# Another layout for the table of relative destinations in a graph-layer kernel, and two short VectorE operations put ahead of a long one

## The chip, the cores and the metric

The kernel runs on one core of a Trainium2 chip. The metric is the device time of one execution in microseconds (us). The kernel before was timed three times: 261.72, 261.30 and 260.92 us, median 261.3 us. Five engines work side by side, each through its own list of instructions in order: TensorE (PE, with its weight loads shown apart as PEld), VectorE (DVE), ScalarE (ACT), GpSimd (POOL) and SyncE (SP), which issues most of the DMA transfers here. They wait for each other through semaphores.

## The reference

The layer adds up edge features by destination node and puts each node through a small network:

```python
recv = edge_index[1]                                  # dst, sorted, 412500 edges
agg = jax.ops.segment_sum(edges, recv, num_segments=12500)   # edges: 412500 x 48
u = graph_globals[batch]                              # batch is 0 for every node
h0 = jnp.maximum(_layernorm(x), 0.0)                  # x: 12500 x 128
h = jax.nn.relu(jnp.concatenate([h0, agg, u], axis=1) @ W1 + b1)   # 240 -> 256
out = x + h @ W2 + b2                                 # 256 -> 128
```

All of it is float32. The edges come sorted by destination, with random counts for each node.

## The kernel before, in words

**Tiling.** The edges are cut into 538 chunks of 768 (128 partitions of 6 consecutive edges each; T = 6 is the place in the partition). Four chunks (CG = 4) make a group and 11 groups (GI = 11) an iteration, which also takes 1024 nodes. There are 12 iterations (NIT), one extra group ahead of them and a rest behind.

**Segment sum by matmuls.** For each edge the kernel keeps its destination relative to the middle of its chunk's window, the table `rel`: one column for each chunk and each of the six places. In each iteration VectorE copies the 264 numbers that it will need (11 groups of 24) from `rel` into the small tile `rel_i` (operation `fr`, in the helper `fetch`), makes one-hot matrices from it by comparing with a row of 28 numbers (`oh0` to `oh5`, in the helper `onehot`, 1344 columns each, one of 672), and TensorE multiplies them with the edge features (`su0` to `su5`, L739). ScalarE copies each result out of its PSUM bank (`ss0` to `ss5`). The results alternate between two banks, so `su5` can only begin when ScalarE has done `ss3`. A second set of one-hots (`pl`) puts the sums at their nodes (`pc`).

**The nodes.** VectorE makes the layer norm's statistics (`st`, `sm`) and shifts (`sh`), ScalarE the normalised rows (`xn`, 8 instructions in an iteration), TensorE turns them (`tu`, L798) and runs the two layers (`hh` L808, `ha` L813, `w2` L834). On ScalarE's list `ss3` stands behind `xn`, and `xn` waits for VectorE's `sh`.

**The start.** Before the loop the destinations are loaded in five blocks of 128 chunks, with a chunk in each partition. VectorE makes them relative (`df`), TensorE transposes them, three places at a time, through three PSUM banks in turn (`td`, L620), and ScalarE copies each turned piece into `rel` (`cd`, L621). The middles of the blocks come from small matmuls (`of`, L613) and two VectorE operations (`vv`, L629, and `off`, L631, in the helper `dst_3`), for block 0 first and for blocks 1 to 4 together later. VectorE also makes the bias (`bj`) from a small matmul (`bi`).

**What sets the order.** Each engine's order is the order in which the program names the operations. A small planner adds the waits: an operation waits for the writers of what it reads, unless its engine already knows of them by a wait for something later on the same engine. What TensorE's loop needs of work ahead of the loop and doesn't learn by its own waits in the loop, it waits for once, at the loop's entry.

Of the kernel before, what the change touches and what calls it, by code (L numbers as in the profile page):

```python
# [18 lines left out]
P = 128  # L19
EPS = 1e-5  # L20
T = 6
CE = P * T
CG = 4
GE = CG * CE
GI = 11
# [29 lines left out]
class Flow:  # L55
# [14 lines left out]
    def op(self, eng, name, reads, writes, emit, dma=False, late=None):  # L70
        self.seq.append(dict(eng=eng, name=name, r=tuple(reads), w=tuple(writes), emit=emit, dma=dma, it=self.at, late=late or {}))
# [350 lines left out]
def kernel(  # L422
# [12 lines left out]
    nc = tc.nc  # L435
# [5 lines left out]
    NIT = E // IE  # L441
    NCH = -(-E // CE)
# [9 lines left out]
    q = CG * T  # L452
# [4 lines left out]
    const = sbufs.enter_context(tc.tile_pool(name="const", bufs=1))  # L457
# [11 lines left out]
    lead = const.tile([P, LEAD], F32)  # L469
    wide = [const.tile([P, len(p) * CG, ROW], F32, name=f"e{s}") for s, p in enumerate(SLOTS)]  # L470
    e = [w[:, :, :T * DE] for w in wide]
    rel = const.tile([P, ((NIT + 1) * GI + 1) * q], F32)
    off = const.tile([P, (NIT + 1) * GI + 1], F32)
    worst = const.tile([P, 3], F32)
    far = const.tile([P, 1], F32)
    farm = const.tile([P, 1], F32)
    rel_i = const.tile([P, GI, q], F32)
    off_i = const.tile([P, GI], F32)
    oh = [const.tile([P, len(p) * q, V], F32, name=f"oh{s}") for s, p in enumerate(SLOTS)]
# [54 lines left out]
    op = f.op  # L534
    A, B, Z = 0, 1, 2

    def dma(eng, name, reads, writes, dst_ap, src_ap):
        def emit(i):
            with nc.allow_non_contiguous_dma(reason="small pieces"):
                return [f.of[eng].dma_start(dst_ap(i) if callable(dst_ap) else dst_ap, src_ap(i) if callable(src_ap) else src_ap)]  # L540
        op(eng, name, reads, writes, emit, dma=True)
# [52 lines left out]
    def dst_shape(b):  # L594
        rows = min(P, NCH - b * P)
        return rows, min(P // CG, NG - b * P // CG), b * P // CG
# [12 lines left out]
    def dst_2(b):  # L609
        rows, n, g0 = dst_shape(b)  # L610
        ob, ok = (ph[1], "PH1") if b else (S[0][:, P:], "S0")
        op("PE", f"of{b}", [f"mf{b}", "aq"], [ok], lambda i: [
            nc.tensor.matmul(ob[:, g0:g0 + n], aq[:rows].rearrange("c k n -> c (k n)"), mf[b][:rows, :n], start=True, stop=True, skip_group_check=True)])  # L613
        dv = df[b % DF].rearrange("c (p t) -> c t p", t=T)
        rv = rel[:, b * P * T:(b * P + rows) * T].rearrange("p (c t) -> p t c", t=T)
        for t0 in range(0, T, 3):
            key, bk = (("PT", pt), ("PH0", ph[0]), ("PO", po))[(2 * b + t0 // 3) % 3]
            pv = bk[:, :3 * P].rearrange("p (t c) -> p t c", t=3)
            op("PE", f"td{b}.{t0}", [f"df{b % DF}", "ident"], [key],
               lambda i, t0=t0, pv=pv: [nc.tensor.transpose(pv[:, t, :rows], dv[:rows, t0 + t, :], ident[:rows, :rows]) for t in range(3)])  # L620
            op("ACT", f"cd{b}.{t0}", [key], [f"rel{b}.{t0}"], lambda i, t0=t0, pv=pv: [nc.scalar.copy(rv[:, t0:t0 + 3], pv[:, :, :rows])])  # L621

    def dst_3(bk, key, some):

        g0 = some[0] * (P // CG)
        n = min(NG, (some[-1] + 1) * (P // CG)) - g0
        vs = [f"vv{b}" for b in some]
        op("DVE", f"vv{some[0]}", [key, "base"], vs, lambda i: [
            nc.vector.tensor_tensor(vv[:, g0:g0 + n], bk[:, g0:g0 + n], flat[:, g0:g0 + n], OP.subtract)])  # L629
        op("DVE", f"of{some[0]}x", vs + ["nmod"], [f"off{b}" for b in some], lambda i: [  # L630
            nc.vector.tensor_scalar(off[:, g0:g0 + n], vv[:, g0:g0 + n], nmod, (WIN - V) / 2, OP.add, OP.add)])  # L631
# [29 lines left out]
    def cols(ap, i, a, n):  # L661
        return ap[:, ds(a(i), n)] if not isinstance(i, int) else ap[:, a(i):a(i) + n]

    def fetch(j):

        it = (f.at or 0) + j
        g0, g1 = it * GI + 1, min(NG, (it + 1) * GI + 1)
        m = GI * CG
        blocks = [b for b in range(NB) if b * P < g1 * CG and (b + 1) * P > g0 * CG]
        rv = rel_i.rearrange("p g t -> p (g t)")  # L670

        op("DVE", "fr", ["relz"] + [f"rel{b}.{t0}" for b in blocks for t0 in (0, 3)], ["rel_i"], lambda i: [nc.vector.tensor_scalar(
            rv, cols(rel, i, lambda i: ((i + j) * GI + 1) * q, m * T), 0.0, None, OP.add)])

    def fetch_off(j):
        it = (f.at or 0) + j
        g0, g1 = it * GI + 1, min(NG, (it + 1) * GI + 1)
        blocks = [b for b in range(NB) if b * P < g1 * CG and (b + 1) * P > g0 * CG]
        op("DVE", "fo", ["offz"] + [f"off{b}" for b in blocks], ["off_i"], lambda i: [nc.vector.tensor_scalar(
            off_i, cols(off, i, lambda i: (i + j) * GI + 1, GI), 0.0, None, OP.add)])  # L680

    def onehot(name, o, reads, r):

        k, n = r.shape[1], r.shape[2]
        ov = o.rearrange("p (k n) v -> p k n v", k=k)
        op("DVE", f"oh{name}", reads + ["iota_v"], [f"oh{name}"], lambda i: [nc.vector.tensor_tensor(  # L686
            ov, iota_v[:, None, None, :].to_broadcast([P, k, n, V]), r[:, :, :, None].to_broadcast([P, k, n, V]), OP.is_equal)])
# [6 lines left out]
    def onehots(s):  # L694
        g = SLOTS[s]
        onehot(s, oh[s], ["rel_i"], rel_i[:, g[0] - 1:g[0]] if len(g) == 1 else rel_i[:, g[0] - 1:g[1]:g[1] - g[0]])
# [149 lines left out]
    def prologue():  # L846
# [12 lines left out]
        pool = lambda name, w, fn, r=(): op("POOL", name, r, w, lambda i: [fn()])  # L859
# [15 lines left out]
        dma("POOL", "lw1b", [], ["w1b"], w1a[HI:HI + DE], W1[D:D + DE])  # L875
        dma("POOL", "lw2", [], ["w2"], w2, W2.rearrange("(a p) d -> p a d", p=P))
        dma("POOL", "lb2", [], ["b2"], b2_sb, b2[None, :].to_broadcast([P, D]))
        pool("relz", ["relz"], lambda: nc.gpsimd.memset(rel[:, NCH * T:], 0.0))

        op("DVE", "c0", [], ["eps", "zero", "worst1", "worst2"], lambda i: [  # L880
            nc.vector.memset(zero, 0.0), nc.vector.memset(eps, EPS), nc.vector.memset(worst, 0.0)])
# [16 lines left out]
        for b in range(NB):  # L898
            dst_1(b)
            dst_2(b)  # L900
        dst_3(S[0][:, P:], "S0", [0])
        onehot(5, oh[5][:, q:], ["rel0.0", "rel0.3"], rel[:, :q].rearrange("p (g t) -> p g t", g=1))
        op("PE", "su5", ["oh5", "e5.1"], ["S1"], lambda i: [
            nc.tensor.matmul(S[1][NV * c:NV * c + V, DE:2 * DE], oh[5][:, (CG + c) * T + t], e[5][:, CG + c, t * DE:(t + 1) * DE],
                             start=(t == 0), stop=(t == T - 1), skip_group_check=True)
# [5 lines left out]
        onehots(1)  # L911
        op("PE", "bi", ["w1u", "u"], ["PH1"], lambda i: [
            nc.tensor.matmul(ph[1][:, NG + a:NG + a + 1], w1u[:, a * P:(a + 1) * P], u, start=True, stop=True, skip_group_check=True) for a in range(NH)])
        onehots(2)
        op("DVE", "bj", ["PH1", "b1"], ["bias"], lambda i: [nc.vector.tensor_tensor(bias, ph[1][:, NG:NG + NH], b1_sb, OP.add)])
        dst_3(ph[1], "PH1", range(1, NB))
        fetch_off(1)
        op("DVE", "spare", [], ["spare"] + [f"di{b}" for b in range(NB)] + [f"di{NB - 1}r", f"di{NB - 1}s"] + [f"df{k}" for k in range(DF)],
           lambda i: [nc.vector.memset(hold[0][:, 0:1], 0.0)])
# [3 lines left out]
            places(s)  # L923
        places_near()
        split("plf", plf, far_, ["off0"], lambda j: off[:, 0:1])
        op("DVE", "f0", ["rel0.0", "rel0.3"], ["farm"], lambda i: [nc.vector.tensor_reduce(farm, rel[:, :q], AX.X, OP.max, apply_absolute_value=True)])

    def body(it):
        f.at = it
# [140 lines left out]
```

## Time and profile before

| | |
|---|---|
| median of three runs | 261.3 us |
| the profiled execution | 261.09 us |
| its span, first to last instruction | 259.3 us |
| PE, DVE, ACT busy | 237.5, 237.4, 128.6 us |
| DMA, mean rate over the span | 364 GB/s |
| from one iteration to the next | 18.16 us |
| `fr`, 264 numbers | 298 ns, 13 times |
| ScalarE's copy of 384 numbers into `rel` | about 0.9 us, 8 times |

The span has three parts: a start to about 34 us, twelve iterations, and an end from about 243 us. Two engines are busy over nine tenths of the time, and the DMA engines move about 390 GB/s through the iterations, so the shares alone do not tell which of them sets the period.

### The profile page before, as it was taken

The numbers are of one execution on the slowest core, as the hardware profiler recorded it, in microseconds if no ns is written. First come the engines' busy times: TensorE is split into PE (matmuls) and PEld (weight loads), VectorE is DVE, ScalarE is ACT, GpSimd is POOL, SyncE is SP. The second block draws the span as 40 slices with busy tenths as digits, with TensorE's granted clock in tenths as the row PEclk, the third lists the DMA queues.
The fourth block names the chain that finished last, engine by engine and source line by source line (L and its number), as shares of the span: only waits on it lengthen the run. The fifth ranks groups of instructions, "written<-read, shape, count | busy, mean of one in ns | idle before, by whom it ended". The sixth has DMA issues, their size and how long they took to land.

```text
span 259.3 us, 17135 instructions
## 1 busy us (share of the span) xinstructions
PE 237.5 (92%) x7539; PEld 185.9 (72%) x7540; DVE 237.4 (92%) x643; ACT 128.6 (50%) x326; POOL 9.1 (4%) x23
## 2 busy tenths in 40 slices
PE   0864889999999999999999999999999999999990
PEld 0854765976967958949859769679589498597680
DVE  5799999999999999999999999999999999999640
ACT  4630454644645536646546446455366465564520
POOL 8200020000000000000000000000000000000000
PEclk9997599999999999999999999999999999999999
DMA  6999999999999999999999999999999999959951
GB/s 215 285 380 388 364 389 391 390 392 390 390 392 390 391 392 390 391 392 390 390 393 390 393 389 391 392 385 388 393 382 389 393 385 390 393 210 350 364 223 65
DMA packets 79012, 94.33 MB, mean 364 GB/s; under 512 B 3227, under 2 KB 72189, under 8 KB 78998
## 3 DMA queue, kind: packets, MB, share of 16 engines
q1 hardware_dynamic: 75398, 87.63, 94.6%
q10 hardware_dynamic: 3312, 6.03, 6.1%
q0 software_dynamic: 288, 0.49, 0.7%
q8 instruction: 7, 0.11, 0.2%
q14 instruction: 7, 0.06, 0.1%
HBM read 87.75 MB, written 6.40 MB: 363 GB/s over the span
## 4 chain that ended last, share of the span: by engine, by line
PE 86%; DVE 6%; DMA 2%; issue 2%; ACT 1%; SPq 0%; DVEq 0%
PE s L739 26%; PE ph L834 17%; PE ph L808 9%; PE ax L761 7%; PE ph L813 5%; PE po L808 4%; PE pt L808 4%; PE pt L813 4%; DVE oh L686 3%; PE pt L798 3%; DMA holda<-in_dst_dram 2%; PE po L798 2%; PE ax L726 2%; DVE pl L692 1%; PE s L992 1%
## 5 line engine op out<-in xcount | busy, mean ns | idle before, releaser
L686 DVE TENSOR_TENSOR oh<-iota_v,rel_i 128x1344 f32<-128x1344 f32 (+1 forms) x78 | 108.6, 1435 | 0.0
L739 PEld LDWEIGHTS s<-e,oh 128*28 128x28 f32 x6336 | 73.0, 110 | 18.3 <-issue 15.9
L739 PE MATMUL s<-e,oh 128*28 128x48 f32 x6336 | 76.9, 211 | 8.1 <-issue 4.6
L743 ACT COPY ss<-s 128x96 f32<-128x96 f32 (+1 forms) x72 | 16.5, 230 | 26.6 <-PE s L739 26.5
L692 DVE TENSOR_SCALAR pl<-iota_w,off_i 128x186 f32<-128x186 f32 x117 | 27.6, 312 | 0.4
L789 ACT ACTIVATE xna<-xa,sha,sca 128x128 f32<-128x128 f32 x48 | 19.8, 482 | 15.9 <-DVE sha L785 15.9
L818 ACT ACTIVATE hida<-ph,bias 128x512 f32<-128x512 f32 x12 | 8.2, 687 | 38.3 <-PE ph L813 38.3
L834 PE MATMUL ph<-w,hida 128*128 128x128 f32 x192 | 24.6, 281 | 0.0
L834 PE MATMUL ph<-w,hidb 128*128 128x128 f32 x192 | 23.4, 275 | 0.0
L834 PEld LDWEIGHTS ph<-w,hida 128*128 128x128 f32 x192 | 22.3, 191 | 0.8
L834 PEld LDWEIGHTS ph<-w,hidb 128*128 128x128 f32 x192 | 22.4, 192 | 0.0
L789 ACT ACTIVATE xnb<-xb,shb,scb 128x128 f32<-128x128 f32 x48 | 19.6, 480 | 0.0
L761 PE MATMUL ax<-pl,ss 128*48 128x186 f32 (+1 forms) x120 | 19.4, 309 | 0.0
L761 PE MATMUL ay<-pl,ss 128*48 128x186 f32 (+1 forms) x120 | 19.4, 309 | 0.0
L761 PEld LDWEIGHTS ax<-pl,ss 128*48 128x48 f32 x120 | 13.8, 123 | 4.7 <-issue 2.0
L799 ACT COPY hta<-pt 128x512 f32<-128x512 f32 x12 | 7.0, 587 | 15.2 <-DVE xbb L793 14.9
L761 PEld LDWEIGHTS ay<-pl,ss 128*48 128x48 f32 x120 | 13.8, 123 | 0.0
L813 PE MATMUL ph<-ags,w1a 48*128 48x512 f32 x48 | 13.5, 641 | 0.0
L808 PE MATMUL ph<-hta,w1h 128*128 128x512 f32 x24 | 13.5, 645 | 0.0
L808 PE MATMUL ph<-htb,w1h 128*128 128x512 f32 x24 | 12.3, 592 | 0.0
L808 PE MATMUL pt<-hta,w1h 128*128 128x512 f32 x24 | 12.3, 592 | 0.0
L808 PE MATMUL po<-htb,w1h 128*128 128x512 f32 x24 | 12.3, 592 | 0.0
(162 smaller groups left out, 334.7 us busy)
## 6 DMA issues: line engine op xcount, KB each, us to landing
e<-in_edge_attr_dram SPq DMA_DIRECT2D x133, 576.0 KB, 9.3
xa<-in_x_dram ACTq DMA_DIRECT2D x11, 256.0 KB, 5.4
xb<-in_x_dram ACTq DMA_DIRECT2D x11, 256.0 KB, 5.5
out_dram<-holda SPq DMA_DIRECT2D x11, 256.0 KB, 3.5
out_dram<-holdb SPq DMA_DIRECT2D x11, 256.0 KB, 3.5
holda<-in_dst_dram SPq DMA_DIRECT2D x4, 384.0 KB, 5.7
e<-in_edge_attr_dram SPq DMA_DIRECT2D x1, 720.0 KB, 6.3
xa<-in_x_dram SPq DMA_DIRECT2D x1, 256.0 KB, 8.8
```

The source lines that it names most:

```text
L686: op("DVE", f"oh{name}", reads + ["iota_v"], [f"oh{name}"], lambda i: [nc.vector.tensor_tensor(ov, iota_v[:, None, None, :].to_broadcast([ ...
L692: nc.vector.tensor_scalar(out[:, j], iota_w, o[j], None, OP.is_equal) for j in range(len(o))])
L739: nc.tensor.matmul(S[k][NV * c:NV * c + V, j * DE:(j + 1) * DE], o[:, (j * CG + c) * T + t], ev[:, j * CG + c, t * DE:(t + 1) * DE], start ...
L743: op("ACT", f"ss{name}", [f"S{k}"], [f"ss{name}"], lambda i: [nc.scalar.copy(sv.rearrange("p j d -> p (j d)"), S[k][:, :m * DE])])
L761: out.append(nc.tensor.matmul(agg[bk][h:h + DE, at:at + w], sv[:, j], pv[:, j, frm:frm + w], start=bk in fresh and bk not in seen, stop=Tr ...
L789: nc.scalar.activation(xn[k][:m, r], xt[k][:m, r], AF.Relu, bias=sh[k][:m, r:r + 1], scale=sc[k][:m, r:r + 1]) for r in range(RR[k])])
L798: op("PE", f"tu{k}", [f"xn{k}", "ident"], [key], lambda i: [nc.tensor.transpose(pv[:, r, :m], xn[k][:m, r], ident[:m, :m]) for r in range( ...
L799: op(eng, f"hT{k}", [key], [f"hT{k}"], lambda i: [copy(hT[k][:, :, :m], pv[:, :, :m])])
L808: nc.tensor.matmul(o, w1h[:, a * P:(a + 1) * P], hT[k][:, :, :m], start=first, stop=False, skip_group_check=True)])
L813: nc.tensor.matmul(o, w1a[h:h + DE, a * P:(a + 1) * P], ag[k // 2][h:h + DE, :, :m], start=False, stop=True, skip_group_check=True)])
L818: nc.scalar.activation(hid[k][:, a, :, :m], o, AF.Relu, bias=bias[:, a:a + 1])])
L834: nc.tensor.matmul(ov[:m, r], hid[k][:, a, r, :m], w2[:, a], start=(a == 0), stop=(a == NH - 1)) for r in range(RR[k]) for a in range(NH)])
```

## The change

`rel` had one long row in each partition in which the six places of a chunk lay side by side. Now it has six rows, one for each place, with the chunks side by side. ScalarE's copies into it so write 128 neighbouring numbers three times, where they wrote every sixth number. `fr` still fills `rel_i` in the old order, and so reads numbers that lie 576 numbers (2304 bytes) apart, six in turn, where it read 264 neighbours. The memset of the unused columns, the first group's one-hot and the first group's maximum read or write the same numbers in the new layout.

Ahead of the loop, `bj` and `dst_3` for blocks 1 to 4 now stand ahead of `onehots(2)`.

```diff
-    rel = const.tile([P, ((NIT + 1) * GI + 1) * q], F32)
+    rel = const.tile([P, T, ((NIT + 1) * GI + 1) * CG], F32)
...
-        rv = rel[:, b * P * T:(b * P + rows) * T].rearrange("p (c t) -> p t c", t=T)
+        rv = rel[:, :, b * P:b * P + rows]
...
-        rv = rel_i.rearrange("p g t -> p (g t)")
+        rv = rel_i.rearrange("p g (c t) -> p (g c) t", t=T)
+        at = lambda i: ((i + j) * GI + 1) * CG
 
         op("DVE", "fr", ["relz"] + [f"rel{b}.{t0}" for b in blocks for t0 in (0, 3)], ["rel_i"], lambda i: [nc.vector.tensor_scalar(
-            rv, cols(rel, i, lambda i: ((i + j) * GI + 1) * q, m * T), 0.0, None, OP.add)])
+            rv, (rel[:, :, at(i):at(i) + m] if isinstance(i, int) else rel[:, :, ds(at(i), m)]).rearrange("p t c -> p c t"),
+            0.0, None, OP.add)])
...
-        onehot(5, oh[5][:, q:], ["rel0.0", "rel0.3"], rel[:, :q].rearrange("p (g t) -> p g t", g=1))
+        onehot(5, oh[5][:, q:], ["rel0.0", "rel0.3"], rel[:, :, :CG].rearrange("p t c -> p c t"))
...
-        onehots(2)
         op("DVE", "bj", ["PH1", "b1"], ["bias"], lambda i: [nc.vector.tensor_tensor(bias, ph[1][:, NG:NG + NH], b1_sb, OP.add)])
         dst_3(ph[1], "PH1", range(1, NB))
+        onehots(2)
...
-        op("DVE", "f0", ["rel0.0", "rel0.3"], ["farm"], lambda i: [nc.vector.tensor_reduce(farm, rel[:, :q], AX.X, OP.max, apply_absolute_value=True)])
+        op("DVE", "f0", ["rel0.0", "rel0.3"], ["farm"], lambda i: [nc.vector.tensor_reduce(farm, rel[:, :, :CG], AX.XY, OP.max, apply_absolute_value=True)])
```

On VectorE, at the start, behind block 0's middles, the kernel before has these rows (`oh_87` to `oh_89` are the one-hots of slots 0 to 2, `bias` is `bj`; what stands in brackets is waited for):

```order
L672 TENSOR_SCALAR rel_i<-rel 128x264 [waits POOL]
L686 TENSOR_TENSOR oh_87<-iota_v,rel_i 128x1344 [waits fr]
L686 TENSOR_TENSOR oh_88<-iota_v,rel_i 128x1344
L686 TENSOR_TENSOR oh_89<-iota_v,rel_i 128x1344
L915 TENSOR_TENSOR bias<-ph_71,b_sb 128x2 [waits lb1,PE]
L629 TENSOR_TENSOR vv<-ph_71,base 128x103
L631 TENSOR_SCALAR off<-vv,nmod 128x103 [waits DVE]
L679 TENSOR_SCALAR off_i<-off 128x11
```

And the changed kernel at the same place:

```order
L673 TENSOR_SCALAR rel_i<-rel 128x264 [waits POOL]
L688 TENSOR_TENSOR oh_87<-iota_v,rel_i 128x1344 [waits fr]
L688 TENSOR_TENSOR oh_88<-iota_v,rel_i 128x1344
L916 TENSOR_TENSOR bias<-ph_71,b_sb 128x2 [waits lb1,PE]
L629 TENSOR_TENSOR vv<-ph_71,base 128x103
L631 TENSOR_SCALAR off<-vv,nmod 128x103 [waits DVE]
L688 TENSOR_TENSOR oh_89<-iota_v,rel_i 128x1344
L681 TENSOR_SCALAR off_i<-off 128x11
```

The three short operations have moved ahead of slot 2's one-hots; the list is otherwise the same.

On TensorE, at the loop's entry and the first sums behind it (`e_74` and `oh_87` belong to slot 0), the kernel before has:

```order
L913 MATMUL ph_71<-u,w1u 128x1 [waits lw1u,lu]
L913 MATMUL ph_71<-u,w1u 128x1
L254 UNCONDITIONAL_BRANCH [waits lw2,lw1h,DVE,lw1b,lw1a]
L257 COMPARE_AND_BRANCH
L739 MATMUL s_65<-e_74,oh_87 28x48 [waits le0_0,oh0]
```

And the changed kernel:

```order
L915 MATMUL ph_71<-u,w1u 128x1 [waits lw1u,lu]
L915 MATMUL ph_71<-u,w1u 128x1
L254 UNCONDITIONAL_BRANCH [waits lw1h,lw2,lw1b,lw1a]
L257 COMPARE_AND_BRANCH
L741 MATMUL s_65<-e_74,oh_87 28x48 [waits le0_0,oh0]
```

The wait for VectorE at the entry is gone: `vv` now stands ahead of slot 2's one-hots, for which TensorE waits inside the loop anyway.

More of the change, by code (lines that the diff above doesn't have):

```diff
@@ L877, in prologue @@
         dma("POOL", "lb2", [], ["b2"], b2_sb, b2[None, :].to_broadcast([P, D]))
-        pool("relz", ["relz"], lambda: nc.gpsimd.memset(rel[:, NCH * T:], 0.0))
+        pool("relz", ["relz"], lambda: nc.gpsimd.memset(rel[:, :, NCH:], 0.0))
         op("DVE", "c0", [], ["eps", "zero", "worst1", "worst2"], lambda i: [
```

## The prediction

> **What bounds the kernel now.** I read the page first, then busy time by iteration, then starts of the same instruction in successive iterations, then the waits, and last the start of the span.
>
> ```profile
> PE 237.5 (92%) x7539; PEld 185.9 (72%) x7540; DVE 237.4 (92%) x643; ACT 128.6 (50%) x326; POOL 9.1 (4%) x23
> ```
>
> PE and DVE are equally busy, so this row doesn't choose. Two whole iterations in the view of stretches (PE, PEld, DVE, ACT, POOL, granted clock, DMA share, GB/s):
>
> ```profile
> 64.93:83.09 18.16, 18.16 (x613) 14.04 (x613) 17.71 (x48) 9.68 (x25) 0.00 (x0) 1.00 1.08 391
> 210.22:228.38 18.16, 18.16 (x614) 14.04 (x613) 17.71 (x48) 9.68 (x25) 0.00 (x0) 1.00 1.08 389
> ```
>
> PE has no idle time in an iteration and DVE 0.45 us. That seems to speak for PE; but ends of matmuls are modelled, so I compare the starts. `far` opens DVE's iteration, `pt` (the turn) is a fixed place on PE; the rows are from the timeline and from the chain of waits:
>
> ```profile
> 24.89 0.41 DVE L635 TENSOR_REDUCE far<-rel_i 128x1 f32<-128x264 f32 x1
> 43.06 0.42 DVE L635 TENSOR_REDUCE far<-rel_i 128x1 f32<-128x264 f32 x1
> 206.52 0.42 DVE L635 TENSOR_REDUCE far<-rel_i 128x1 f32<-128x264 f32 x1
> 53.27 0.59 PE pt L798 x4
> 216.72 0.58 PE pt L798 x4
> ...
> 27.22 1.81 PE L739 MATMUL s<-e,oh 128*28 128x48 f32 x77 [3.91 <-issue]
> ```
>
> DVE takes 18.17 us for its first iteration (24.89 to 43.06), in which PE stood idle for 3.91 us and more, and (206.52 - 24.89) / 10 = 18.163 us on the mean. PE takes (216.72 - 53.27) / 9 = 18.161. DVE doesn't go faster where it has PE to itself: 18.16 us is the length of its own list, and the 0.45 us are gaps between dependent instructions. Two engines that keep one period to 2 ns over ten iterations are tied. The waits of 62 to 243 us hold no row in which DVE or PE matmuls wait; of the ties this is the one that runs from DVE:
>
> ```profile
> ACT xna L789 <- DVE sha L785: 13.3, 10, 1.3
> ```
>
> Behind `xna` and `xnb` ScalarE copies `ss3`, and `su5` on PE may not start before it, as it writes the same bank. Where the copy of one iteration ends, in stretches of 0.1 us (PE, PEld, DVE, ACT):
>
> ```profile
> 51.78 0.21 ACT L743 COPY ss<-s 128x96 f32<-128x96 f32 x1
> ...
> 51.84:51.94 0.10, 0.10 (x29) 0.10 (x19) 0.00 (x0) 0.10 (x1) 1.00 1.12 403
> 51.94:52.04 0.10, 0.10 (x25) 0.10 (x11) 0.00 (x0) 0.06 (x1) 1.00 1.05 380
> 52.04:52.14 0.10, 0.10 (x23) 0.10 (x15) 0.00 (x0) 0.00 (x0) 1.00 1.08 392
> 52.14:52.24 0.10, 0.10 (x23) 0.10 (x20) 0.00 (x0) 0.00 (x0) 1.00 1.09 392
> ```
>
> The weight loads fall from 19 to 11 exactly as the copy ends at 51.99: PE stops for a few hundredths of a us for `ss3`. So DVE sets the period, through `sh`, ScalarE's eight `xn` and `ss3`; PE is faster by a hair only. **Whatever DVE's list gains in an iteration the period gains in full; what it loses brings almost nothing.**
>
> At the start the same path opens PE's unbroken run:
>
> ```profile
> 30.31 0.16 DVE L785 SCALAR_TENSOR_TENSOR sha<-sma,sca 128x4 f32<-128x4 f32 x1
> 30.51 1.65 ACT L789 ACTIVATE xna<-xa,sha,sca 128x128 f32<-128x128 f32 x4 [1.20 <-DVE sha L785]
> 33.61 0.31 ACT L743 COPY ss<-s 128x96 f32<-128x96 f32 x2
> 33.87 1.23 PE L739 MATMUL s<-e,oh 128*28 128x48 f32 x96 [0.92 <-ACT ss L743]
> ```
>
> From 11.17 to 30.31 us DVE's rows follow one another without a wait, so the start, too, is as long as DVE's list.
>
> **The change part by part.**
>
> *`fr` reads at a distance.* It is in DVE's list 13 times ahead of the last `sh`: once before the loop and once in each of 12 iterations. DVE's groups by shape (count, then total busy us and mean ns):
>
> ```profile
> L672 DVE TENSOR_SCALAR rel_i<-rel 128x264 f32 x12 | 3.6, 298 | 0.0
> L679 DVE TENSOR_SCALAR off_i<-off 128x11 f32 x12 | 2.1, 173 | 0.4
> L635 DVE TENSOR_REDUCE far<-rel_i 128x1 f32<-128x264 f32 x13 | 5.5, 420 | 0.0
> L892 DVE TENSOR_REDUCE m<-ident 128x32 f32<-128x128 f32 x1 | 0.3, 276 | 0.0
> L894 DVE TENSOR_REDUCE a<-ident 128x4 f32<-128x128 f32 x1 | 0.4, 366 | 0.0
> ```
>
> From L679 to L672, 253 more numbers cost 125 ns: 0.49 ns each, or two in 0.99 ns. The reduces go one by one: 136 more numbers cost 144 ns, 1.06 ns each. L892 and L894 sum the same 128 numbers, L892 neighbours, L894 with a step of 4 numbers (16 bytes): 90 ns more, 0.70 ns for each number that is not beside the last one. The trace has no such read in a tensor_scalar, so I bound it. Below: the distance is free, 298 ns. Above: `fr` falls to one number at a time and each pays the hop, 173 + 253 x (1.06 + 0.70) = 618 ns, 320 more. A dearer hop than L894's would go higher still, but no row here shows one in an SBUF read. Between: one number at a time with no price for hops, 173 + 253 x 1.06 = 441, 143 more; or two at a time with one hop's price for the pair, 132 x 0.70 = 93 more, 391 ns. [...] 13 x 0.093 = **+1.2 us**. Nothing covers it: `fr` stands ahead of `sh` in DVE's order, `xn`, `ss3` and `su5` come later by as much, and PE's own lead is a few hundredths.
>
> [...]
>
> *ScalarE's copies write neighbours.* ScalarE's groups:
>
> ```profile
> L621 ACT COPY rel<-ph 128x384 f32<-128x384 f32 x3 | 2.7, 912 | 0.0
> L799 ACT COPY hta<-pt 128x512 f32<-128x512 f32 x12 | 7.0, 587 | 15.2 <-DVE xbb L793 14.9 <-PE pt L798 0.3
> L743 ACT COPY ss<-s 128x96 f32<-128x96 f32 x60 | 14.2, 236 | 23.6 <-PE s L739 23.6
> ```
>
> Contiguous copies cost (587 - 236) / 416 = 0.84 ns for a number, so 384 should take 479 ns: some 0.43 us less for each of eight. They free the three banks sooner, for PE's later transposes. DVE's one wait on that path is this:
>
> ```profile
> 7.50 0.62 PE L613 MATMUL s<-mf,aq 128*128 128x32 f32 x2 [7.50 <-DVE fc L603]
> 8.86 0.85 ACT L621 COPY rel<-pt 128x384 f32<-128x384 f32 x1 [4.89 <-PE pt L620]
> 10.21 0.85 PE L620 MATMUL pt<-ident,holda 128*128 128x128 f32 x3
> 11.17 0.61 DVE L606 TENSOR_SCALAR holda<-holda,fc 26x768 f32<-26x768 int32 x1 [0.50 <-PE pt L620]
> ```
>
> PE comes to these transposes without a pause from 7.50 us on, and the bank's first copy (8.86 + 0.85 = 9.71) is long done at 10.21. So the wait stays: **0**. If it did fall away it would be worth its 0.50 us.
>
> *`bj`, `vv`, `off` ahead of slot 2's one-hots.* The same instructions in another order: **0** for DVE, if `bj` has not to wait for its matmuls:
>
> ```profile
> 13.30 4.50 DVE L686 TENSOR_TENSOR oh<-iota_v,rel_i 128x1344 f32<-128x1344 f32 x3
> 15.54 0.60 PE L913 MATMUL ph<-u,w1u 64*128 64x1 f32 x4
> 17.72 0.15 DVE L915 TENSOR_TENSOR bias<-ph,b_sb 128x2 f32<-128x2 f32 x1
> 18.27 0.17 DVE L679 TENSOR_SCALAR off_i<-off 128x11 f32<-128x11 f32 x1
> 18.70 1.62 PE L739 MATMUL s<-e,oh 128*28 128x48 f32 x84 [2.55 <-DVE vv L629]
> 20.00:25.00 5.00, 2.59 (x141) 2.25 (x130) 5.00 (x17) 0.48 (x2) 0.00 (x0) 0.75 1.09 393
> ```
>
> Its matmuls end at 15.54 + 0.60 = 16.14. A set of one-hots takes (17.72 - 13.30) / 3 = 1.47 us, so `bj` would come at 17.72 - 1.47 = 16.25, plus `fr`'s 0.09. The margin is 0.2 us, and the faster copies can only widen it. What is delayed, slot 2's one-hots, ends at 16.34 + 0.55 + 1.47 = 18.4, and `su2` stands behind `su0` and `su1`. PE drops its 2.55 us wait for `vv` and starts `su0` about 2 us sooner. But the first place where PE's time reaches the end is `su5` behind `ss3` at 33.87, which DVE sets: **0**. The loads that `su0` to `su2` let go are no gain either: the DMA engines move 393 GB/s at that time with what was issued before (the last row, a stretch of 5 us).
>
> *The small readers.* The first group's one-hot and maximum read 24 numbers from `rel`: 24 x 0.70 = 17 ns at most each, once. GpSimd's memset fills the same 228 numbers:
>
> ```profile
> 7.45 0.61 POOL L878 MEMSET rel<- 128x228 f32 x1
> 12.98 0.29 DVE L672 TENSOR_SCALAR rel_i<-rel 128x264 f32<-128x264 f32 x1
> ```
>
> It ends at 8.06, 4.9 us before `fr` needs it, and would have to take nine times as long to be seen. **0**.
>
> The sum against the profiled execution (span 259.3 and 1.8 around it, 261.1): +1.2, 262.3. The median of the runs is 0.2 above it: **262.5 us**, 0.5% slower.
>
> **The rivals.**
>
> *1. `fr` one number at a time.* With hops, 13 x 0.320 = +4.2, **265.5 us**; without, 13 x 0.143 = +1.9, 263.2. For it: the source now has two dimensions that don't merge, and no row shows a stepped source at two numbers a time. Against it:
>
> ```profile
> L895 DVE COPY aq<-a 128x128 f32<-128x128 f32 x1 | 0.2, 226 | 0.0
> ```
>
> This copy's source has two dimensions as well (4 numbers, each repeated 32 times), and its 226 ns for 128 numbers are less than the 276 of L892's one by one. [...]
>
> *2. The distance is free* and nothing else moves: DVE's list keeps its length and the time stays at **261.3 us**, on the other side of my forecast. It decides if `fr` costs under 0.78 / 13 = 0.06 us more. For it: hops could hide where two numbers come at once; against it, L894's 90 ns, on the same engine.
>
> *3. The start is shorter and `fr` free.* If DVE's 0.50 us wait at 11.17 goes, or PE's earlier sums let `ss3` out sooner, 260.8 us. Against it: PE's unbroken run there, and `ss3` is held by `xn`, not by `su3`. That the period itself shrinks needs a shorter DVE list, and the change shortens nothing there.
>
> **How the numbers follow.** Forecast 0.48; rival 1 0.28, of which 0.13 with hops and 0.15 for what lies between it and the forecast; rival 2, 0.18; rival 3, 0.06. A measurement of this kernel tells about 0.3%, 0.8 us, from no change. Of the forecast's 0.48 some 0.07 may come out under that. Slower: 0.41 + 0.28 = 0.69. Same: 0.07 + 0.16 = 0.23. Faster: 0.08, with what is left of rivals 2 and 3. The range goes from rival 2 (261.2) to rival 1 with hops (265.6).
>
> **What would show it.** `fr`'s row first: near 390 ns for the forecast, 298 for rival 2, 440 or 620 for rival 1. Then `far` to `far`: 18.16 plus the same difference; if the period grows by less, DVE was not the bound. PE should show small waits for `ss` in the iterations. ScalarE's copies into `rel` near 0.48 us, PE's first sums near 17 us, with `sha` at 30.31 plus two times `fr`'s difference and not earlier. An `fr` over 0.65 us, a wait of `bj`, or a period under 18.15 us would make me wrong.

## The result and the profile after

The changed kernel takes **262.97 us**, the median of 21 runs (262.07 to 263.70), against 261.62 for the kernel before (21 runs beside it, 260.76 to 263.26): a ratio of 1.0042, with a 95% interval of 1.0025 to 1.0059. It is slower by 1.35 us where 1.2 were predicted. The profiled execution took 262.77 us with a span of 261.0.

VectorE's and ScalarE's groups by shape in the changed kernel (count, then total busy us and mean ns):

```profile
L673 DVE TENSOR_SCALAR rel_i<-rel 128x264 f32 x12 | 4.7, 394 | 0.0
L621 ACT COPY rel<-ph 128x384 f32<-128x384 f32 x3 | 1.4, 478 | 0.3 <-PE ph L620 0.3
```

`fr` went from 298 to 394 ns, 96 more; ScalarE's copies fell from 912 to 478. Now the instructions that the prediction named, in the changed kernel's timeline:

```profile
24.75 0.42 DVE L635 TENSOR_REDUCE far<-rel_i 128x1 f32<-128x264 f32 x1
30.26 0.16 DVE L787 SCALAR_TENSOR_TENSOR sha<-sma,sca 128x4 f32<-128x4 f32 x1
61.81 0.42 DVE L635 TENSOR_REDUCE far<-rel_i 128x1 f32<-128x264 f32 x1
226.15 0.42 DVE L635 TENSOR_REDUCE far<-rel_i 128x1 f32<-128x264 f32 x1
```

VectorE's list takes (226.15 - 61.81) / 9 = 18.260 us an iteration, 0.10 more than before, as `fr` says. So far all is as forecast. The turns on TensorE, from the chain of waits of the changed kernel, tell something else:

```profile
35.96 1.05 PE pt L800 x4
54.95 0.59 PE pt L800 x4
...
236.53 0.59 PE pt L800 x4
```

Before, the second stood at 53.27, and the first and the last were:

```profile
35.10 0.59 PE pt L798 x4
...
234.88 0.59 PE pt L798 x4
```

The last one is 1.65 us later, and all of that was lost by the second turn, which is 1.68 later. From the second turn to the last TensorE needs (236.53 - 54.95) / 10 = 18.158 us, no more than before. So in this execution TensorE was late at the start and then kept its own pace, while VectorE's longer list caught up with it. The distance between the two is seen on ScalarE, in the second and in the last iteration of the changed kernel's timeline (`xnb`, and `ss3` behind it):

```profile
50.82 1.63 ACT L791 ACTIVATE xnb<-xb,shb,scb 128x128 f32<-128x128 f32 x4
53.43 0.24 ACT L745 COPY ss<-s 128x96 f32<-128x96 f32 x1 [0.98 <-PE s L741]
...
233.44 1.64 ACT L791 ACTIVATE xnb<-xb,shb,scb 128x128 f32<-128x128 f32 x4
235.02 0.24 ACT L745 COPY ss<-s 128x96 f32<-128x96 f32 x1
```

In the second iteration `ss3` waits for TensorE and ends 53.67 - 52.45 = 1.22 us behind `xnb`; in the last it ends 235.26 - 235.08 = 0.18 us behind it. VectorE's way to `ss3` eats up about 0.1 us of the distance in each iteration and arrives at the tie as the loop ends.

Why was TensorE late? A stretch of the changed kernel's start (PE, PEld, DVE, ACT, POOL, granted clock, DMA share, GB/s):

```profile
34.30:37.60 3.30, 3.30 (x92) 3.03 (x84) 3.23 (x5) 0.56 (x2) 0.00 (x0) 0.50 1.09 390
```

And one of the kernel before:

```profile
34.30:37.70 3.40, 3.40 (x108) 2.94 (x97) 3.33 (x4) 1.17 (x3) 0.00 (x0) 1.00 1.08 390
```

The granted clock was still half there, where before it was full. Behind the same wait for `ss3`, `su5` and the turns ran at half speed, in the changed kernel's timeline:

```profile
33.82 2.14 PE L741 MATMUL s<-e,oh 128*28 128x48 f32 x96 [2.23 <-ACT ss L745]
35.89 1.12 PE L800 MATMUL pt<-ident,xna 128*128 128x128 f32 x4
```

`su5` took 1.23 us before, the four turns of `xna` 0.66. So two things could carry the loss: VectorE's longer list, or a clock that came late. One profile can't tell which; the experiments can.

### The profile page after: what moved, and what is told of

The parts are those of the page before. It is cut to its first block, busy times and chain, and to the rows that moved or that the text cites. A ratio compares the mean times of both kernels' runs of the same rounds, so it can differ in the third digit from the quotient of the medians.

```text
span 261.0 us, 17135 instructions
## 1 busy us (share of the span) xinstructions
PE 239.1 (92%) x7539; PEld 187.1 (72%) x7540; DVE 239.4 (92%) x643; ACT 127.7 (49%) x326; POOL 7.9 (3%) x23
## 4 chain that ended last, share of the span: by engine, by line
PE 85%; DVE 6%; DMA 3%; issue 2%; ACT 1%; SPq 1%; DVEq 0%
PE s L741 26%; PE ph L836 17%; PE ph L810 9%; PE ax L763 7%; PE ph L815 5%; PE po L810 4%; PE pt L810 4%; PE pt L815 4%; DVE oh L688 3%; PE pt L800 3%; DMA holda<-in_dst_dram 3%; PE po L800 2%; PE ax L728 2%; SPq L540 1%; DVE pl L694 1%
## 5 line engine op out<-in xcount | busy, mean ns | idle before, releaser
L741 PEld LDWEIGHTS s<-e,oh 128*28 128x28 f32 x6336 | 74.1, 111 | 19.5 <-issue 14.7
L741 PE MATMUL s<-e,oh 128*28 128x48 f32 x6336 | 78.3, 212 | 8.9 <-issue 5.7
```

Source lines behind the costliest of these rows:

```text
L741: nc.tensor.matmul(S[k][NV * c:NV * c + V, j * DE:(j + 1) * DE], o[:, (j * CG + c) * T + t], ev[:, j * CG + c, t * DE:(t + 1) * DE], start ...
```

## The experiments

My theory: the layout carries the loss, through `fr`'s hops (reads from one distant number to the next) in VectorE's list. The rival: the new order of the start lets TensorE idle at another place, its clock comes late, and that is the loss; that the one brings the other is a guess of mine. All ratios are against the kernel before.

**The two parts apart.** The order alone, with the old layout:

```diff
-        onehots(2)
         op("DVE", "bj", ...)
         dst_3(ph[1], "PH1", range(1, NB))
+        onehots(2)
```

> The old layout with the new order at the start. Theory F (the time was lost in fr: 0.1 us more in each of 13 places of VectorE's list, which sets the period): nothing moves, within 0.3% of before, fr 298 ns, far to far 18.16 us. Rival C (the time was lost at the start: TensorE's sums come earlier, it is idle in other places, and the clock is granted at half until about 37 us as in the changed kernel's profile, where it was full again at 32.8 before): about 1.0 to 1.7 us slower than before, with the period unchanged.

Measured: 261.58 us (12 runs) against 261.38, a ratio of 1.0009, 0.998 to 1.0038. The order costs nothing that can be seen, though the interval would still hold up to 1.0 us. Its values run from 260.68 to 263.48, and the profile fell on the highest of them. Its turns, from the chain of waits:

```profile
36.26 1.05 PE pt L798 x4
55.61 0.58 PE pt L798 x4
237.25 0.59 PE pt L798 x4
```

With the old `fr` (297 ns) the late start appears as well, with a granted clock of 0.50 from 28 to 37 us and 0.70 on the mean from 37 to 40, and then again TensorE's own pace, (237.25 - 55.61) / 10 = 18.164 us. A late clock is thus no property of the layout. The layout alone, with the old order:

```diff
+        onehots(2)
         op("DVE", "bj", ...)
         dst_3(ph[1], "PH1", range(1, NB))
-        onehots(2)
```

(against the changed kernel)

> The new layout with the old order at the start. Theory F: all of the loss, 1.2 to 1.4 us over before, fr 0.39 us, far to far 18.26 us. Rival C: within 0.3% of before, since TensorE's first sums wait for VectorE's middles as they did; or a part of the loss, if ScalarE's shorter copies already change where TensorE is idle.

Measured: 262.68 us, a ratio of 1.0048, 1.0021 to 1.0075, and no run under 262.34. In its profile the clock was full in time (1.00 from 34 us on), and the chain of waits shows the mechanism of the prediction undisturbed:

```profile
71.78 0.59 PE pt L800 x4
236.19 0.58 PE pt L800 x4
```

From 71.78 to 236.19 an iteration takes 18.268 us on TensorE, too. `fr` took 411 ns there, and `ss3` (the second row, in its timeline) ends right behind `xnb` in every iteration:

```profile
233.16 1.63 ACT L791 ACTIVATE xnb<-xb,shb,scb 128x128 f32<-128x128 f32 x4
234.70 0.22 ACT L745 COPY ss<-s 128x96 f32<-128x96 f32 x1
```

The distance is 234.92 - 234.79 = 0.13 us: this is the tie at which VectorE holds TensorE. TensorE's weight loads show the hold itself. In stretches of 0.1 us, with the instructions on the tile `s` alone (length, PE, PEld, DVE, ACT, granted clock, DMA share, GB/s), there are about 19 loads in a stretch, but where `su5` begins there are 6 and 8, here in one iteration:

```profile
106.94:107.04 0.10, 0.10 (x19) 0.05 (x6) 0.00 (x0) 0.09 (x1) 1.00 1.18 426
107.04:107.14 0.10, 0.10 (x13) 0.06 (x8) 0.00 (x0) 0.00 (x0) 1.00 1.08 392
```

The rival falls for the loss as a whole: the layout alone has all of it.

**The changed kernel and the one before, profiled once more.** No edit.

> The changed kernel once more, for a second profile of it. In the first one TensorE's clock was at half until 37.6 us, its first turn came 0.9 us late, and from the second turn on it kept its own 18.16 us, with VectorE's list of 18.26 catching up from behind. If that was one way of several in which the same program runs, this profile may show the other, as e2's did: the clock full by about 33 us, ss3 right behind xnb in every iteration, turns 18.26 us apart, and a span of 260.3 to 260.9. If TensorE holds the end in every execution of the changed kernel, the turns are 18.16 us apart again.

> The kernel before once more, for a second profile. About a quarter of its executions lie near 263 us. If this one does, its profile should show the clock at half beyond 33 us and first turns 1 to 2 us late, as e1's did; if it lies near 261.3, first turn to second turn is 18.2 us, or 18.7 if slot 2's one-hots of the first iteration took 2.08 us.

Measured: 262.80 us and 261.28 us, one run each. The second profile of the changed kernel shows both mechanisms, one after the other, in its chain of waits:

```profile
35.86 0.59 PE pt L800 x4
54.02 0.59 PE pt L800 x4
72.18 0.58 PE pt L800 x4
...
218.32 0.58 PE pt L800 x4
236.60 0.59 PE pt L800 x4
```

TensorE starts late (35.86), does 18.16 us twice, then VectorE's list has caught up and sets 18.27 to 18.29 to the end. The last turn comes at 236.60, within 0.07 us of the first profile's, in which TensorE was later and VectorE never held it. The second profile of the kernel before had a first turn at 35.30 and took 18.16 to 18.18 us in every iteration. Slot 2's one-hots of its first iteration took 2.09 us, for which I had expected 18.7 in the first step; but its VectorE list had begun 0.44 us earlier and its TensorE 0.20 us later than in the first profile, and the first step took 18.16 all the same.

These profiles also settle that neither the layout nor the order is needed for a late clock. It is full again at 37.6 and at 35.7 us in the two profiles of the changed kernel, at 32.8 and at 34.9 in those of the kernel before: the same program differs by 2 us.

So the time is the later of two ways: TensorE's start plus iterations at its own pace, and VectorE's list. It fits what the two kernels' values show: the lowest of 21 goes up from 260.76 to 262.07, as the longer list says, but the highest only from 263.26 to 263.70, because where TensorE is late the list has room to catch up. That high values are late clocks is shown for the profile of the order alone (263.48); for the highest values of the kernel before it is argued.

**`fr` in runs of four.** `rel_i` takes the places first and the chunks second within a group, so that `fr` reads four neighbours at a time; the readers of the one-hots take the new places.

```diff
-        rv = rel_i.rearrange("p g (c t) -> p (g c) t", t=T)
+        rv = rel_i.rearrange("p g (t c) -> p g t c", t=T)
...
-            rv, (...).rearrange("p t c -> p c t"),
+            rv, (...).rearrange("p t (g c) -> p g t c", c=CG),
```

> The whole change, but rel_i keeps the places of a group first and its four chunks second, so that fr reads runs of four neighbours (16 bytes) and only the order of the columns within a group's one-hots changes. Theory F: fr falls to about 300 ns if a run of four is as cheap as neighbours (330 if each run's start costs 0.7 ns), far to far is 18.16 us again, and the time is before's within 0.3%. Rival C: the time stays where the change left it, 1.0 to 1.7 us over before.

Measured: 263.00 us, 1.0054 (1.0029 to 1.0080): a miss. Its group:

```profile
L673 DVE TENSOR_SCALAR rel_i<-rel 128x264 f32 x12 | 5.1, 428 | 0.0
```

428 ns are near what I had worked out for one number at a time without a price for hops (441). The hops were gone, but the two at a time, too. What this view has and the changed kernel's not is an odd number outside: 11 groups, against 44 chunks. So, the same data with the six places outside (the new chunk order of `rel_i` stays):

```diff
-        rv = rel_i.rearrange("p g (t c) -> p g t c", t=T)
+        rv = rel_i.rearrange("p g (t c) -> p t g c", t=T)
...
-            rv, (...).rearrange("p t (g c) -> p g t c", c=CG),
+            rv, (...).rearrange("p t (g c) -> p t g c", c=CG),
```

(against the kernel with runs of four)

> As e3, but fr runs over the six places outside and the 44 chunks inside: it reads six runs of 44 neighbours and writes runs of four. In e3 fr took 428 ns, what 264 numbers cost one at a time without a price for hops (441), so the runs of four were free and the two at a time were lost. Theory F2 (a tensor_scalar takes two at a time only where the outermost dimension is even or merges; e3's is 11, this one's is 6): fr 300 to 330 ns, far to far 18.16 to 18.19 us, and the time within 0.3% of before. Rival (any second dimension in the old or new tile costs about 0.1 us): fr 390 to 430 ns and 1.2 us over before.

Measured: 261.99 us against 261.57, 1.0003 (0.9971 to 1.0034). Its group:

```profile
L673 DVE TENSOR_SCALAR rel_i<-rel 128x264 f32 x12 | 3.6, 298 | 0.0
```

With ScalarE's neighbouring writes and the new order kept, `fr` is back at 298 ns, and the list at 18.157 us an iteration (`far` at 61.42 and nine iterations later at 224.83). The interval is wide, but the lowest of the twelve values is 260.79, under every one of the changed kernel's (262.07 and up). With the layout's own run this says that `fr`'s price is the loss; the interval leaves room for up to 0.9 us.

**The price by itself.** Eleven copies from `rel` into `rel_i`, one after the other behind the loop of the kernel before (m is 44 chunks, T 6 places; a name tells the step, `r4` and `r2` are 144 numbers in runs of four and of two, 24 apart):

```diff
+        some = [("base", flat, rel[:, :m * T]),
+                ("s576", flat.rearrange("p (c t) -> p c t", t=T), rows(m)),
+                ("s576odd", flat[:, :43 * T].rearrange("p (c t) -> p c t", t=T), rows(43)),
+                ("s2", flat, step(2, m * T)), ("s4", flat, step(4, m * T)), ("s6", ...), ("s12", ...),
+                ("s24", flat[:, :144], step(24, 144)), ("b144", flat[:, :144], rel[:, :144]),
+                ("r4", ...), ("r2", ...)]
```

> The kernel before with eleven more VectorE copies (tensor_scalar, plus zero) at its end, from its table into rel_i after its last use, to price the hop by itself; the time of the whole doesn't count. Theory F2 in ns: 264 neighbours 300; 44 x 6 with a step of 576 numbers inside 390; 43 x 6 the same way, odd outside, 580 to 620 (one at a time, each with its hop); one number in 2, 4, 6, 12: 300 to 310 for 2, and 390 or more from 4 on; 144 neighbours 240; one in 24, 144 times, 290 or more; runs of four and of two, 24 apart, 144 numbers: 240. Rival (the second dimension itself costs 0.1 us): one in 4, 6 and 12 stay at 300, and the two copies in runs cost as much more as the 44 x 6.

The rows of this kernel's timeline, in the order of the diff (the steps of 6 and 12, 0.40 us each, are left out):

```profile
250.57 0.29 DVE L995 TENSOR_SCALAR rel_i<-rel 128x264 f32<-128x264 f32 x1
250.90 0.39 DVE L995 TENSOR_SCALAR rel_i<-rel 128x264 f32<-128x264 f32 x1
251.32 0.61 DVE L995 TENSOR_SCALAR rel_i<-rel 128x258 f32<-128x258 f32 x1
251.96 0.30 DVE L995 TENSOR_SCALAR rel_i<-rel 128x264 f32<-128x264 f32 x1
252.30 0.41 DVE L995 TENSOR_SCALAR rel_i<-rel 128x264 f32<-128x264 f32 x1
...
253.61 0.34 DVE L995 TENSOR_SCALAR rel_i<-rel 128x144 f32<-128x144 f32 x1
253.99 0.23 DVE L995 TENSOR_SCALAR rel_i<-rel 128x144 f32<-128x144 f32 x1
254.25 0.23 DVE L995 TENSOR_SCALAR rel_i<-rel 128x144 f32<-128x144 f32 x1
254.52 0.25 DVE L995 TENSOR_SCALAR rel_i<-rel 128x144 f32<-128x144 f32 x1
```

The changed kernel's read costs 0.10 us over neighbours (0.39 against 0.29). With 43 chunks outside in place of 44, fewer numbers take 0.61 us, 0.22 more: that is what one number at a time, each with its hop, was to cost, the prediction's upper bound (618 ns). A step of two is nearly free (0.30), steps of 4, 6, 12 and 576 cost about the same (0.41, 0.40, 0.40, 0.39), a step of 24 more (0.34 against 0.23 for 144 numbers, 0.11 / 72 = 1.5 ns a pair against 0.10 / 132 = 0.76). Runs of four and of two cost 0 to 0.02.

So among these copies the two at a time goes with an even count outside: 44 gave 0.39 us, 43 gave 0.61, though 43 x 6 = 258 numbers are even as well, and in the loop 11 gave 428 ns where six gave 298. With the prediction's 0.99 ns for a pair of neighbours a pair takes 1.75 ns at the step of 576 and 2.5 at the step of 24; why the step of 24 costs more isn't shown.

**VectorE's list made shorter.** The changed kernel without the running maximum (`far`) in the loop, so that the list loses more than `fr` added:

```diff
-        farthest()
         fetch(1)
```

> The changed kernel without the running maximum of the relative places in the loop (two VectorE operations, 0.62 us of VectorE's list in each iteration; the kernel leaves out that part of its check of the inputs). VectorE's list then lasts 18.26 - 0.62 = 17.64 us, so it can't set the period, and what is left is TensorE's own pace. Theory F: TensorE's own period is shorter than 18.16 us by a few hundredths at most, and the time is before's or up to 0.3 us below it. Rival C: the start still costs its half clock, and the time stays 1.0 to 1.7 us over before.

Measured: 260.50 us (260.27 to 260.84, and one run of 261.97) against 261.38, 0.9968 (0.9943 to 0.9993). Its chain of waits:

```profile
34.66 0.59 PE pt L800 x4
52.84 0.58 PE pt L800 x4
234.45 0.59 PE pt L800 x4
```

(234.45 - 52.84) / 10 = 18.161 us: with VectorE out of the way this is TensorE's own period, and it equals the one before, (234.88 - 53.27) / 10 = 18.161. What this execution gained came at the start, once: 0.44 us at the first turn. The median gained 0.88 us where at most 0.3 was expected; the rest isn't accounted for. The weight loads where `su5` begins, as above:

```profile
87.79:87.89 0.10, 0.10 (x29) 0.10 (x16) 0.00 (x0) 0.10 (x1) 1.00 1.15 415
87.89:87.99 0.10, 0.10 (x24) 0.10 (x15) 0.00 (x0) 0.00 (x0) 1.00 1.15 415
```

So a small dip is there where VectorE holds nothing, too; the 6 and 8 of the layout alone are the hold.

**The tie.** In the changed kernel `far` goes behind the statistics and `sh` ahead of `fr` and of the one-hots, so that `fr` is no longer on the way from `far` to `ss3`:

```diff
-        farthest()
-        fetch(1)
         add_slots(0, 1)
...
+        farthest()
+        shift(A)
+        shift(B)
+        fetch(1)
         add_slots(2)
         onehots(0)
-        shift(A)
-        shift(B)
```

> The changed kernel with fr still at 0.39 us, but in each iteration sh now stands ahead of fr and of slot 0's one-hots: 1.5 to 2 us earlier in VectorE's list, which stays as long. Theory F with sh, xn and ss3 as the only way from VectorE to TensorE: the list of 18.26 us falls back 0.1 us an iteration against a lead of over 1.2 us and never catches up, the period is TensorE's 18.16, and the time is at or under before's, 260.7 to 261.4. Rival (there is a second way that is nearly as tight, by xbb, the issue of the x loads on ScalarE behind it, and the copies of the turns behind that): the period is again 18.26 us and the time 0.8 to 1.2 us over before's, as in the changed kernel.

Measured: 263.32 us against 261.66, 1.0056 (1.0036 to 1.0076). That is 1.66 us more, over the 0.8 to 1.2 that I had named for a second way. `ss3` now had over a microsecond of room, and nothing was won. The waits of 62 to 243 us of this kernel show another way from VectorE:

```profile
ACT hta L801 <- DVE xbb L795: 18.9, 9, 2.2
```

And its timeline, in one iteration:

```profile
72.66 0.69 DVE L795 TENSOR_TENSOR xbb<-xb,b_sb 128x512 f32<-128x512 f32 x1
73.38 0.34 ACTq L540 DMA_DIRECT2D xb<-in_x_dram  x1
73.76 0.59 ACT L801 COPY hta<-pt 128x512 f32<-128x512 f32 x1 [2.09 <-DVE xbb L795]
```

ScalarE issues the load of the next `xb`, which has to wait until VectorE has read the old one in `xbb`, and `hta`, which TensorE needs for `hh`, stands behind that issue. `hta` ends at 74.35 here and `hh` begins at 74.40. Before, that row of waits was 12.2 us in nine times, and in the same iteration `hta` ended at 73.70, 0.57 us ahead of `hh` at 74.27: the way was there, with that much room. The list itself was 18.37 us, 0.11 longer than the changed kernel's with the same instructions; why stays open.

**What makes the start vary.** In the changed kernel's first iteration slot 2's one-hots took 2.08 us instead of 1.55. The rows of VectorE and GpSimd there, in the changed kernel's timeline:

```profile
31.70 1.06 POOL L795 TENSOR_TENSOR xbr<-xr,b_sb 106x256 f32<-106x256 f32 x1 [23.96 <-DMA xr<-in_x_dram]
32.09 2.08 DVE L688 TENSOR_TENSOR oh<-iota_v,rel_i 128x1344 f32<-128x1344 f32 x1
```

And in the timeline of the kernel before:

```profile
32.15 1.55 DVE L686 TENSOR_TENSOR oh<-iota_v,rel_i 128x1344 f32<-128x1344 f32 x1
32.40 1.89 POOL L793 TENSOR_TENSOR xbr<-xr,b_sb 106x256 f32<-106x256 f32 x1 [24.33 <-DMA xr<-in_x_dram]
```

Whichever begins second ends late: GpSimd's sum took 1.89 us where it was second and 1.06 where it was first, VectorE's one-hots 2.08 and 1.55. In the other profiles, too, the one-hots took 2.08 or 2.09 us wherever the sum had begun ahead of them, and 1.55 elsewhere. For GpSimd the price is less clear: its sum took 0.79 to 1.84 us where it began first and 1.89 to 2.02 where second, and its spans are rough. GpSimd's sum begins when a load has landed, so this varies from execution to execution; in the second profile of the kernel before the one-hots took 2.09 us. Both pairs of rows say that the second one pays; by how much isn't that plain, as the one-hots lost 0.53 us and the sum ran on for 0.67 beside them. What the two share isn't shown. To take this collision away, the kernel before with the sum on VectorE, behind the loop:

```diff
-        add_b(Z, m, "POOL")
+        add_b(Z, m)
```

> The kernel before with one operation moved: the sum of the rest's x and b2 is done by VectorE behind the loop, not by GpSimd at about 32 us. In the profiles of the changed kernel, e1, e2 and e4 GpSimd's sum began ahead of slot 2's one-hots in the first iteration and they took 2.08 us, in those of before and e3 it began behind and they took 1.55. If the two share a way into the memory, VectorE's list loses up to 0.53 us in some of the executions and none in others: without the sum the one-hots always take 1.55, and the median is 0 to 0.5 us under before's. If the 0.53 us have another cause they come again, and the median stays.

Measured: 261.11 us against 261.57, 0.9991 (0.9962 to 1.0019). The one-hots took 1.55 us, eight of twelve runs lie within 260.89 to 261.18, the other four at 262.18 to 262.94. The collision may spread the lower values by some tenths; it isn't what makes the upper ones. For these, the kernel before with more matmuls at the start, to see whether the clock comes up earlier:

```diff
-    f.brief = {f"w2{k}": lambda i, k=k: [nc.tensor.matmul(ph[k][:, 0:1], ...)] for k in (A, B)}
+    f.brief = {f"w2{k}": lambda i, k=k: [nc.tensor.matmul(ph[k][:, 0:1], ...)]
+               + [nc.tensor.matmul(ph[k][:, 128:128 + H], hid[k][:, 0, 0], w1h, ...) for _ in range(2)] for k in (A, B)}
```

> The kernel before with four more TensorE matmuls of 256 columns at about 29 us, in the short branch that stands for w2 in the first iteration (they multiply zeros and nothing reads them). In the profiles of the changed kernel and of e1 TensorE's clock was granted at half until 37.6 and 38.8 us, and su5 and the turns of the first iteration took 0.9 and 1.2 us longer; in that of before it was full from 32.8 on. If TensorE's idle time at 24 to 34 us holds the clock down in some executions (those of before near 263 us), the added work removes those, and the highest are near 261.7. If not, the spread stays, or all become up to 1.5 us slower, because the added work itself delays su3 to su5.

Measured: 264.44 us (263.35 to 265.89, 11 runs), 1.0094 (1.0063 to 1.0124): a miss. A part of it is that the added work itself was in the way, as `ss3` in its timeline shows:

```profile
34.59 0.24 ACT L743 COPY ss<-s 128x96 f32<-128x96 f32 x1 [1.00 <-PE s L739]
```

It now waits for TensorE, a microsecond later than before (33.61), and VectorE's last instruction ends 1.02 us later than before, at 254.63. But this execution's span is 3.6 us longer (262.9 against 259.3). The other 2.6 us lie behind that instruction: from its end to the end of the span it is 8.3 us here and 5.7 in the kernel before, for which no cause is shown. The clock was full from 33.4 us on in this profile, and the turns of `xna` took 0.66 us as in the kernel before, so it shows nothing of a late one. What keeps the clock at half stays open.

**A version that beats both.** The new layout and order with the places outside, and, on top of that kernel: the running maximum behind `xbb`, where it no longer stands ahead of `sh` (the first iteration's numbers are looked through once behind the loop), and the sum of `xbr` on VectorE behind the loop:

```diff
-        farthest()
         fetch(1)
...
             add_b(k)
+        farthest()
...
+        op("DVE", "fa0", [], ["far"], lambda i: [nc.vector.tensor_reduce(far, rel[:, :, CG:(GI + 1) * CG], AX.XY, OP.max, apply_absolute_value=True)])
...
-        add_b(Z, m, "POOL")
+        add_b(Z, m)
```

> e5 (fr at 298 ns in the new layout) with two operations moved: GpSimd's sum goes to VectorE behind the loop, as in e7, and the running maximum stands behind xbb in the iteration instead of ahead of fr (the first iteration's numbers are checked once behind the loop), so that VectorE's list is as long as before, but sh of the first iteration comes 0.62 us sooner. Theory F (VectorE's list sets where TensorE's unbroken run begins; afterwards both take 18.16 us): as in e4 the first turn is 0.4 to 0.5 us earlier, the period 18.16, and the time 0.8 to 1.1 us under before's median, 260.4 to 260.8. Rival (e4's gain came from the work left out in every iteration): no more than e7's gain, 0 to 0.5 us under before.

Measured: 260.60 us (260.04 to 261.39) against 261.66, a ratio of **0.9939**, 0.9919 to 0.9960. Its first turn is at 34.76, 0.34 us earlier than before, its iterations take TensorE's 18.16 us, VectorE's list has 18.07, and none of twelve values lies near 263. VectorE's list is 0.09 us shorter than I had worked out, for which I have no reason. How much each edit gives wasn't tried apart on this kernel.

## Why the prediction was right, and where not

**`fr` (+93 ns, two at a time with one hop's price): right.** 96 ns in the profile of the changed kernel, 84 to 113 in the others with this `fr`. The reason held as well: the copies by themselves put two at a time with the hop at 0.39 us, and one at a time with the hop at 0.61. That `fr` would keep two at a time was my estimate: no row of the kernel before shows a tensor_scalar with a stepped source. In these copies it went with the outermost count, not with that of all numbers: 44 outside kept it, 43 outside (258 numbers) lost it, and with 264 numbers and 11 outside `fr` lost it, at 428 ns. That this layout has 44 outside was luck.

**The sum (+1.2 us): right.** The layout alone has +1.30 us and the changed kernel +1.35, and 13 x 0.096 is 1.25; with the places outside no loss is seen. In the layout's profile TensorE's way also runs through slot 2's one-hots of the first iteration while they take 2.08 us. The kernel before meets that collision, too, but how often either kernel does isn't measured, so that all of the 1.30 is `fr`'s is not shown. That the changed kernel's first profiled execution came out as far over the one before as it did (262.77 against 261.09) was chance: there it was the late clock that lost the time.

**"Whatever DVE's list gains in an iteration the period gains in full": right as a limit, too simple as an account.** It is what happens in the layout's profile, and in the second profile of the changed kernel from the fourth turn on. In its first profile the period on TensorE was 18.158 us to the end, and the 1.7 us had come from half a clock in the first iteration. I had looked at TensorE's lead in an iteration and not at where it may start. The lead is not "a few hundredths": TensorE's own period is VectorE's to 1 or 2 ns, so either may hold the other, and the start decides which. The dip in the weight loads that I read as TensorE stopping for `ss3` (19, 11, 15) was no proof: an iteration later the kernel before has 16 and 15, without `far` it is the same, and where VectorE held TensorE there were 6 and 8.

**"What it loses brings almost nothing": right for the iteration, wrong for the start.** Without `far` the period stayed at 18.161 us, but the first turn came 0.44 us earlier, and the median is 0.9 us lower. The best version lives on that.

**The path through `sh`, `xn`, `ss3`: right, but not the only one.** With `sh` ahead, TensorE is held through `xbb`, ScalarE's issue of the next load and `hta`, which had 0.57 us of room before.

**The reorder (0): right.** 1.0009 for it alone, within its interval. Of the three short operations (`bj`, `vv`, `off`), `bj` came at 16.11 and had not to wait. TensorE's first sums came at 14.78 us and not near 17: with its wait for `vv` gone it only needed `oh0`. That was 1.9 us more than I had worked out, and worth nothing, as said.

**ScalarE's copies (0): right.** 478 ns, worked out as 479. VectorE's wait for TensorE at 11.17 us did go away in the changed kernel's profile, against the prediction, but waits for loads of `dst` vary beside it: 0.73 us before, 1.17 (at 8.62) after. It isn't the copies: the order alone, with the old copies, has no wait for TensorE there, and the layout alone has one of 0.39 us.

**The signs.** `fr`, the list and the copies came as named. `sha` was to be at 30.31 plus two times `fr`'s difference and not earlier; it was at 30.26. Its way from `far` is 30.26 - 24.75 = 5.51 us, 0.09 more than before, but the list began 0.14 earlier. And I had expected waits of TensorE for `ss`: the lists of waits have none, even where VectorE does hold it; the places of the turns tell, and the weight loads in stretches of 0.1 us.

**The rivals.** One number at a time (rival 1) is refuted for this `fr` (394 ns) and shown for an odd count outside (0.61 us with 43). A free hop (rival 2) is refuted here (96 ns) and nearly true for runs of four and of two (0.23 and 0.25 us against 0.23). A shorter start (rival 3) is not what this change does, but 0.4 us were there to be had.

## What to carry to other kernels

When two engines show the same period, find out what each would take alone (shorten the other's list), and where each starts: the time is the later of two ways, and one profile may show either. A copy on VectorE that gathers from a distance kept two numbers at a time here where the outermost count was even (0.39 us for 44 x 6, 0.61 for 43 x 6), and paid next to nothing for the distance where each run had two neighbours (0.25 us against 0.23); the order of the dimensions in the view is worth as much as the layout (298 ns against 428 for the order, 298 against 394 for the layout). A small sum on GpSimd was not free beside VectorE's one-hots: they took 2.08 us instead of 1.55.

## What the runs showed of the hardware

- The granted clock stayed at half until 37.6 us in one execution and was full from 32.8 us in another, in nearly the same program; in the late one the second turn came 1.68 us later (54.95 against 53.27). The same program differs by 2 us from one execution to the next (37.6 and 35.7, 32.8 and 34.9). In the starts of two profiles its changes lie whole multiples of 3.4 us apart: in that of the kernel before at 19.13, 22.54, 25.96 and 32.78 us (3.41, 3.42 and 6.82 apart), in that of the changed one at 17.15 and 37.62 (20.47, six times 3.41). What in the start makes it late isn't shown here.
- GpSimd's sum and VectorE's one-hots get in each other's way: the one-hots took 2.08 us instead of 1.55 where the sum had begun first, the sum 1.89 to 2.02 us where the one-hots had.
- In these copies VectorE's two at a time goes with the outermost count: 0.61 us for 43 x 6 numbers, 0.39 for 44 x 6.
- ScalarE writing every sixth number takes 912 ns for 384, neighbours 478.
